# Four edits to the last stage of a two-layer kernel: where its scatters, its tile rows, its turned states and its filling products stand

## The chip, the cores and the metric

The kernel runs on one core of a Trainium2 chip. A core has a matrix engine (PE, with its weight loads listed apart as PEld), a vector engine (DVE), a scalar engine (ACT), a general engine (POOL) and an engine that only issues transfers (SP). Each works through its own instructions in order, and they wait for each other through semaphores. The metric is the device time of one execution in microseconds, as the median of several runs.

## The reference

The reference is a model of two layers on x of 8 x 512 x 256 (all fp32): conditioning, attention, a recurrence and a mixture of heads in the first, an adaptive low-rank block, causal attention, a second recurrence and a layer of experts in the second. Only the last two matter here; the input of this stage is x after everything else, and its output is added to x.

```python
# second recurrence: 512 steps, 8 rows, 256 states
xW = jnp.einsum('ntd,dh->nth', x, Wx) + b
def step(h_prev, xw_t):
    h_next = jnp.tanh(xw_t + h_prev @ Wh)
    return (h_next, h_next)
_, hs = jax.lax.scan(step, h0, jnp.swapaxes(xW, 0, 1))
x = jnp.swapaxes(hs, 0, 1)
# experts: 16, the best two of each row, and a shared one
router_logits = jax.nn.sigmoid(x @ gate_w + gate_b)
expert_values, expert_indices = jax.lax.top_k(router_logits, k=2)
expert_values = expert_values / jnp.sum(expert_values, axis=-1, keepdims=True)
hg = jnp.einsum('bsd,edi->bsei', x, experts_wg)
hu = jnp.einsum('bsd,edi->bsei', x, experts_wu)
all_outputs = jnp.einsum('bsei,eid->bsed', jax.nn.silu(hg) * hu, experts_wd)
selected = jnp.take_along_axis(all_outputs, expert_indices[..., None], axis=2)
return x + mlp(x, shared_wg, shared_wu, shared_wd) + jnp.sum(expert_values[..., None] * selected, axis=2)
```

## The kernel before

The last stage is the function `rnn_moe`. One loop over t = 0 to 511 emits a step of the recurrence and, beside it, a piece of the work on rows that are done. The order of PE, ACT and DVE is written out by that loop; the order of POOL and SP is left to the scheduler of the tile framework.

A step (`rnn_step`) is: 8 small products of the state with Wh into one of two accumulators `M.pg` (L1446; the 256 outputs stand in four strips of 32 partitions, 64 columns each, so the four run side by side); the tanh on ACT (L1448); a turn of 32 x 32 blocks on DVE into a ring of 16 steps (L1449), which is the state operand of the next step. `rnn_seed` (L1430) starts the next accumulator with the projected input: it picks the 8 rows of step t+1 with columns of the identity, four products. All seeds stand on PE between the state products of one step and those of the next, and behind the other products of that step.

Beside a step the loop calls four queues of generators, each advanced by one `yield` in a step. `ranks` and `gathers` are advanced in every step. Of `chunks` and `big` one is advanced: `chunks` first, and `big` if that gave 0. A `yield 1` says that products were emitted, a `yield 0` that none were. A step in which both give 0 is called empty here; in it the seeds are emitted three times in place of once.

What the queues hold, in order of time:

- `rnn_project` (`big`, first 62 steps): the projections x @ Wx of 16 steps, one 256-wide product in a step (L1411).
- `chunk` (every 16 steps): 128 finished rows. POOL copies the ring into hT; two turns pass; then logits of the router and the turned states `hr` (L1500, L1502), the shared expert (L1516, L1525, L1538) and the residual (L1542).
- `rank` (after 9, 9, 9 and 5 chunks, a block): sorts the rows by expert, with each expert's rows in whole tiles of 128; then 18 scatters of a block (10 in the last), each an indirect DMA from POOL of 128 rows of `hr` into `M.xs` (L1627). Each is ordered behind the turn of the step in which it is emitted (`paced`). After four more turns `tiles` goes into `big`.
- `tiles`: 33 tiles in a block (25 in the last). `fetch` copies an expert's weights on POOL (L1657, L1658) and loads 128 rows from `M.xs` on SP (L1660); the first four are fetched at once, the others four tiles ahead. A tile takes three steps: two gate products (L1673), then the down product of the tile before (L1689) with the turn of the rows two tiles on (L1665). The results go to `M.ys` (L1694).
- `collect`: indirect DMAs from POOL that gather rows from `M.ys` (L1725), their weighted sum (L1733) and the output. There is one gather in every three or four steps, and after the loop two in three.

When the loop over t ends, what is left in the queues is emitted without steps in between: the tail. M.pace, behind which gathers and scatters are ordered, is then the last down product.

Of the kernel before, what the change touches and what calls it, by code (L numbers as in the profile page):

```python
# [10 lines left out]
F32 = mybir.dt.float32  # L11
I32 = mybir.dt.int32
U32 = mybir.dt.uint32
AF = mybir.ActivationFunctionType
# [5 lines left out]
P = 128  # L20
B = 8
S = 512
D = 256
# [51 lines left out]
def load_kp(nc, pool, src, name, n, k=2, eng=None):  # L75

    t = pool.tile([P, k, n], F32, name=name)
    (eng or nc.sync).dma_start(out=t, in_=src.rearrange("(k p) n -> p k n", p=P))
    return t
# [295 lines left out]
class Edges:  # L375
# [3 lines left out]
    NE = E // P  # L379
# [1000 lines left out]
XB = 16  # L1380
# [42 lines left out]
        yield 0  # L1423


def rnn_seed(K, M, t, closed=False):

    pick = K.ident.rearrange("p (b t) -> p t b", b=B)
    for j in range(4):
        K.nc.tensor.matmul(  # L1430
            M.pg[t % 2][32 * j : 32 * j + B], pick[:, t % XB, :], M.xw[:, t // XB, 64 * j : 64 * j + 64], start=True, stop=closed
        )


def rnn_step(K, M, t):


    nc, mm = K.nc, K.nc.tensor.matmul
    at = t % XB
    if at == 0:  # L1440
        M.last, M.ring = M.ring, M.rg.tile([P, XB, 2, 32], F32, name="ring", tag="ring")
    pg = M.pg[t % 2]
    for k in range(2):
        hp = K.h0T[:, k, :] if t == 0 else (M.ring[:, at - 1, k, 0:B] if at else M.last[:, XB - 1, k, 0:B])
        for j in range(4):
            mm(pg[32 * j : 32 * j + B], hp, M.wh[:, k, 64 * j : 64 * j + 64], start=False, stop=(k == 1))  # L1446
    h = M.hp.tile([P, 64], F32, name="h", tag="h")
    nc.scalar.activation(h, pg, AF.Tanh)  # L1448
    M.pace = nc.vector.transpose(M.ring[:, at].rearrange("p k b -> p (k b)"), h)  # L1449


class Experts:
# [9 lines left out]
    NE = 16  # L1462
# [20 lines left out]
    def chunk(self, c, ring):  # L1483

        K, M, NE = self.K, self.M, self.NE
        nc, mm, later = K.nc, K.nc.tensor.matmul, M.later
        t0 = (self.first + c) * XB
        hT = M.hp.tile([P, 2, B, XB], F32, name="hT", tag="hT")
        for k in range(2):
            nc.gpsimd.tensor_copy(hT[:, k], ring[:, :, k, 0:B].rearrange("p t b -> p b t"))  # L1490
        for n in range(2):
            saved_x(K, M, t0 // XB + n)
        xc = M.saved[t0 // XB]
        hk = [hT[:, k].rearrange("p b t -> p (b t)") for k in range(2)]
        yield 0
        yield 0
        ph = M.pd.tile([P, D + NE], F32, name="ph", tag="pd")
        pr, pt = ph[:, D : D + NE], ph[:, 0:D]
        for k in range(2):
            mm(pr, hk[k], M.wr[:, k, :], start=(k == 0), stop=(k == 1))  # L1500
        for k in range(2):
            nc.tensor.transpose(pt[:, k * P : (k + 1) * P], hk[k], K.ident)  # L1502
        rl = M.sp.tile([P, NE], F32, name="rl", tag="rl")
        hr = M.ap.tile([P, D], F32, name="hr", tag="hr", bufs=16)
        self.hr.append(hr)

        def turned():
            nc.vector.tensor_tensor(rl, pr, M.rb, ALU.add)
            nc.scalar.activation(rl, rl, AF.Sigmoid)
            nc.scalar.copy(hr, pt)  # L1510

        later(turned)
        yield 1
        pw = M.pgu.tile([P, 2, P], F32, name="pw", tag="gu")
        for k in range(2):
            mm(pw[:, 0], M.wg[:, k, :], hk[k], start=(k == 0), stop=(k == 1))  # L1516

        def first():
            nc.vector.max(out=self.top[:, c, :], in_=rl)
            nc.vector.max_index(out=self.topi[:, c, :], in_max=self.top[:, c, :], in_values=rl)  # L1520

        later(first)
        yield 1
        for k in range(2):
            mm(pw[:, 1], M.wu[:, k, :], hk[k], start=(k == 0), stop=(k == 1))  # L1525
        a = M.sp.tile([P, P], F32, name="a", tag="a")

        def act():
            nc.scalar.activation(a, pw[:, 0], AF.Sigmoid)
            nc.vector.tensor_tensor(a, pw[:, 0], a, ALU.mult)  # L1530
            nc.vector.tensor_tensor(a, pw[:, 1], a, ALU.mult)

        later(act)
        yield 1
        yield 0
        yield 0
        pd = M.pd.tile([P, D], F32, name="pd", tag="pd")
        mm(pd, a, M.wd, start=True, stop=False)  # L1538
        yield 1
        pj = pd.rearrange("p (j k r) -> p k j r", j=4, k=2)  # L1540
        for k in range(2):
            mm(pj[:, k], xc[:, k], K.ident, start=False, stop=(k == 1))  # L1542
        acc = M.ap.tile([P, D], F32, name="acc", tag="acc", bufs=27)
        self.acc.append(acc)
        later(
            lambda: nc.vector.tensor_tensor(
                acc.rearrange("p (j k r) -> p j k r", j=4, k=2),
                pd.rearrange("p (j k r) -> p j k r", j=4, k=2),
                hr.rearrange("p (k j r) -> p j k r", j=4, k=2),
                ALU.add,  # L1550
            )
        )
        yield 1

    def rank(self):

        K, M, NE, NT, C, rp, top = self.K, self.M, self.NE, self.NT, self.C, self.rp, self.top
        nc, mm = K.nc, K.nc.tensor.matmul
# [66 lines left out]
        for c in range(C):  # L1625
            for i in range(2):
                w = nc.gpsimd.indirect_dma_start(  # L1627
                    out=self.xs[:, :],
                    out_offset=bass.IndirectOffsetOnAxis(ap=self.row[:, c, i : i + 1], axis=0),
                    in_=self.hr[c],  # L1630
                    in_offset=None,
                )
                self.paced(w)
                K.tc.declare_no_dep(w.ins, group=group, reason="rows of their own")
                K.tc.add_to_no_dep_group(group, w.ins)
                yield 0

    def tiles(self):

        K, M, NT = self.K, self.M, self.NT  # L1640
        nc, mm, later = K.nc, K.nc.tensor.matmul, M.later
# [11 lines left out]
        def fetch(m):  # L1653
            if m % 4 == 0:
                whose(m)
            e, W[m] = bass.ds(W[m], 1), M.wp.tile([P, 768], F32, name="w", tag="w")
            nc.gpsimd.tensor_copy(W[m][:, 0 : 2 * D], M.wgu[:, e, :].rearrange("p o n -> p (o n)"))  # L1657
            nc.gpsimd.tensor_copy(W[m][:, 2 * D : 3 * D], M.wdn[:, e, :].rearrange("p o n -> p (o n)"))  # L1658
            X[m] = M.sp.tile([P, D], F32, name="x", tag="x", bufs=6)
            nc.sync.dma_start(out=X[m], in_=self.xs[m * P : (m + 1) * P, :])  # L1660
# [36 lines left out]

        for m in range(4):
            fetch(m)
        for m in range(2):  # L1700
            turn(m)
            yield 1
# [38 lines left out]
def rnn_moe(K, out):  # L1741


    nc, inp = K.nc, K.inp
    with ExitStack() as es:
        wp = K.pool(es, "m_w")
# [13 lines left out]
        M.wh = load_kp(nc, wp, inp["rnn_wh"], "wh", 256)  # L1760
        M.rbias = wp.tile([P, D], F32, name="rbias")
        nc.sync.dma_start(out=M.rbias, in_=inp["rnn_b"].partition_broadcast(P))
        M.wr = load_kp(nc, wp, inp["gate_w"], "wr", 16)
        M.rb = wp.tile([P, 16], F32, name="rb")
        nc.sync.dma_start(out=M.rb, in_=inp["gate_b"].partition_broadcast(P))
        M.wg = load_kp(nc, wp, inp["shared_wg"], "wg", P)
# [19 lines left out]
        M.hp = K.pool(es, "m_h", 2)  # L1786
        M.psx = K.pool(es, "m_px", 1, PSUM)
        psg = K.pool(es, "m_pg", 1, PSUM)
        M.pg = [psg.tile([P, 64], F32, name=f"pg{i}") for i in range(2)]
        for t in M.pg:  # L1790
            nc.vector.memset(t, 0.0)
        M.pxt = K.pool(es, "m_xt", 1, PSUM)
        M.pgu = K.pool(es, "m_gu", 2, PSUM)
        M.pd = K.pool(es, "m_pd", 2, PSUM)
# [27 lines left out]

        def ranked(x):
            yield from x.rank()
            for _ in range(4):
                yield 0
            big.append(tiled(x))

# [11 lines left out]
        with K.tc.manual_schedule(engines={E.PE, E.Activation, E.DVE}):  # L1840
            for t in range(S):
                if t % XB == 0:
                    if t == XB * sum(BLOCKS[: nb + 1]):
                        nb += 1
                        block, at = Experts(K, M, nb), 0
                rnn_step(K, M, t)
                consume()
                advance(ranks)
                advance(gathers)
                idle = not (advance(chunks) or advance(big))  # L1850
                if t + 1 < S:
                    for i in range(2 * idle, -1, -1):
                        rnn_seed(K, M, t + 1, i > 0)
                if t % XB == XB - 1:
                    chunks.append(chunk(block, at, M.ring))
                    at += 1
            while chunks or ranks or big or gathers:
                consume()
                M.left = bool(chunks or ranks or big)
                advance(ranks)  # L1860
                advance(gathers)
                if advance(chunks) or advance(big):
                    M.pace = M.last
            consume()
# [171 lines left out]
```

## Time and profile before

| | |
|---|---|
| median of 10 runs | 4029.07 us (4020.14 to 4034.01) |
| the profiled execution | 4028.14 us, span 4026.0 us |
| the last stage's loop, first to last turn (L1449) | 3227.42 to 3881.91 us |
| the tail | 3881.91 to 4026 us |
| busy in the whole span | PE 3517.3, PEld 2437.5, DVE 2337.2, ACT 1523.4, POOL 666.7 us |
| mean granted PE clock | 0.976 |

How to read it: a busy time is that of an engine with an instruction in it; PE's records overlap, since matmuls are pipelined and their ends are modelled, so the start of one record to the start of the next is the better measure. An fp32 product of the common form stands as two records, a transpose as one. A line of the timeline has the start and the duration in us, the engine, the line of the kernel, the operation with its output and inputs, how many records were merged, and in brackets the idle time before it and what ended that. In a table by stretch the columns are the stretch, its length, the busy time of each engine with the number of instructions, the granted PE clock (1.00 is full speed), the busy share of the DMA engines and GB/s.

### The profile page before, as it was taken

To read this page: it belongs to the slowest core of one execution; us is meant where nothing else is said; L and a number is where in the kernel's file an instruction comes from. 1 tells how busy PE (TensorE), PEld (TensorE's weight loads), DVE (VectorE), ACT (ScalarE), POOL (GpSimd) and SP (SyncE) were. 2 spreads that over 40 slices of the span, in tenths; PEclk is the share of its full clock that TensorE was granted. 3 is DMA by queue.
4 is the path that set the end of the run, shared out by engine and by line. 5 is a ranking of instruction groups with operands and counts; after the bars stand their busy time and mean duration, and the time that the engine had idled before them with its cause. 6 is when DMAs were issued, how large, how long until landed. Compare 5 with 4: busy or idle time off the path is not lost.

```text
span 4026.0 us, 152559 instructions
## 1 busy us (share of the span) xinstructions
PE 3517.3 (87%) x66340; PEld 2437.5 (61%) x66340; DVE 2337.2 (58%) x8334; ACT 1523.4 (38%) x5283; POOL 666.7 (17%) x1370
## 2 busy tenths in 40 slices
PE   8999888888888887599888999999998897898986
PEld 5533566666666666466555666666666665666665
DVE  4488666666666666466656666666666533233334
ACT  3111233334333333355444444444444322232333
POOL 1000000000000000111022222222222110233356
PEclk9999999999999999899999999999999999999998
DMA  3122000000000000100000000000000060222235
GB/s 107 43 72 70 24 16 21 21 16 16 5 4 4 4 4 33 55 17 25 2 1 1 1 1 1 1 1 1 1 1 1 1 197 31 68 67 89 73 121 152
DMA packets 100814, 138.13 MB, mean 34 GB/s; under 512 B 13152, under 2 KB 81664, under 8 KB 99760
## 3 DMA queue, kind: packets, MB, share of 16 engines
q1 hardware_dynamic: 85264, 88.80, 7.1%
q0 software_dynamic: 12064, 34.34, 2.7%
q8 instruction: 520, 8.52, 0.9%
q10 hardware_dynamic: 2816, 5.24, 0.4%
q14 instruction: 150, 1.23, 0.1%
HBM read 86.26 MB, written 43.25 MB: 32 GB/s over the span
## 4 chain that ended last, share of the span: by engine, by line
PE 65%; DVE 17%; ACT 12%; issue 4%; DMA 1%; POOL 1%; another core or an unknown queue 0%; SPq 0%; POOLq 0%; ACTq 0%; DVEq 0%
PE pgi L669 8%; PE pe L1223 4%; PE pg L1446 4%; PE pp L1183 4%; DVE G L675 4%; PE pt L1266 3%; PE po L1281 3%; PE U L489 3%; PE pg L1673 3%; PE px L1298 3%; PE pk L468 3%; ACT X L676 3%; ACT th L686 3%; DVE pr L682 2%; PE pg L1430 2%
## 5 line engine op out<-in xcount | busy, mean ns | idle before, releaser
L669 PE MATMUL pgi<-wh,ring 128*8 128x128 f32 x8176 | 318.6, 274 | 207.6 <-DVE ring L687 206.8
L669 PEld LDWEIGHTS pgi<-wh,ring 128*8 128x8 f32 x8176 | 171.2, 88 | 378.3 <-DVE ring L687 377.7
L1449 DVE STREAM_TRANSPOSE ring<-h 128x64 f32<-128x64 f32 x512 | 125.6, 245 | 424.4 <-ACT h L1448 410.6
L1243 ACT ACTIVATE sm<-sm,nm 128x388 f32<-128x388 f32 (+3 forms) x512 | 284.0, 556 | 175.0 <-DVE nm L1239 174.6
L676 ACT ACTIVATE X<-G 128x32 f32<-128x32 f32 x512 | 117.1, 229 | 597.1 <-DVE G L675 597.1
L675 DVE STREAM_TRANSPOSE G<-pgi 128x128 f32<-128x128 f32 x512 | 162.7, 318 | 233.5 <-PE pgi L669 233.5
L1448 ACT ACTIVATE h<-pg 128x64 f32<-128x64 f32 x512 | 114.7, 224 | 481.4 <-PE pg L1446 421.8
L1183 PE MATMUL pp<-hn,wqkv 128*128 128x512 f32 x512 | 251.3, 636 | 30.4 <-ACT oT L1282 29.5
L1446 PE MATMUL pg<-wh,ring 128*8 128x64 f32 x8176 | 215.3, 223 | 62.5 <-DVE ring L1449 50.3
L1266 PE MATMUL pt<-ident,sm 128*128 128x128 f32 x1280 | 189.9, 281 | 74.0 <-DVE sm L1249 61.7
L1250 POOL COPY pme<-sm 128x4 f32<-128x4 f32 x512 | 120.3, 235 | 759.5 <-DVE sm L1249 755.6
L1266 PEld LDWEIGHTS pt<-ident,sm 128*128 128x128 f32 x1280 | 147.8, 143 | 155.2 <-issue 93.7
L1268 ACT COPY eT<-pt 128x512 f32<-128x512 f32 (+1 forms) x192 | 105.6, 550 | 352.4 <-PE pt L1266 351.0
L630 POOL COPY xc<-xT 128x128 f32<-128x128 f32 x64 | 17.1, 296 | 1184.5 <-DVE xT L552 1184.5
L669 PE MATMUL pgo<-wh,ring 128*8 128x64 f32 x8176 | 208.1, 219 | 1.9 <-issue 1.9
L669 PE MATMUL pgg<-wh,ring 128*8 128x64 f32 x8176 | 207.7, 219 | 0.0
L648 PE MATMUL pgi<-xw,ident 128*8 128x128 f32 x4096 | 206.2, 273 | 0.0
L1239 DVE CUSTOM_DVE_ANT_0 sm<-pe,mask 128x260 f32<-128x260 f32 (+2 forms) x384 | 141.7, 425 | 90.0 <-PE pe L1223 89.7
L1446 PEld LDWEIGHTS pg<-wh,ring 128*8 128x8 f32 x8176 | 137.3, 91 | 87.3 <-DVE ring L1449 71.7
L1183 PEld LDWEIGHTS pp<-hn,wqkv 128*128 128x128 f32 x512 | 97.9, 201 | 150.3 <-issue 101.5
L636 PE MATMUL px<-wx,xc 128*128 128x256 f32 x512 | 178.7, 433 | 5.0 <-POOL xc L630 5.0
L1673 PE MATMUL pg<-xT,w 128*128 128x128 f32 x992 | 166.4, 300 | 18.6 <-issue 7.3
(496 smaller groups left out, 8148.5 us busy)
## 6 DMA issues: line engine op xcount, KB each, us to landing
cb<-order POOLq DMA_DIRECT2D x32, 512.0 KB
x<-xs SPq DMA_DIRECT2D x124, 128.0 KB
ys<-y SPq DMA_DIRECT2D x124, 128.0 KB
xs<-zero SPq DMA_DIRECT2D x66, 128.0 KB
w<-in_ada_w_dram SPq DMA_DIRECT2D x16, 512.0 KB
w<-in_moh_w_dram SPq DMA_DIRECT2D x32, 192.0 KB
xres<-xp SPq DMA_DIRECT2D x32, 128.0 KB
xc<-xres SPq DMA_DIRECT2D x32, 128.0 KB
```

What stands on the lines that cost most here:

```text
L636: mm(px, xc[:, k], wx[:, k, c], start=(k == 0), stop=(k == 1))
L648: mm(dst[32 * j : 32 * j + B], pick[:, t % XB, :], xw[:, j * 256 + lo : j * 256 + hi], start=True, stop=False)
L669: mm(dst[32 * j : 32 * j + B], hp, wh[:, k, j * 256 + lo : j * 256 + hi], start=False, stop=(k == 1))
L675: nc.vector.transpose(G[:, 0:2].rearrange("p g k b -> p (g k b)"), pgi[t % 2].rearrange("p g n -> p (g n)"))
L676: nc.scalar.activation(X[:, 0:2], G[:, 0:2, :, 0:B], AF.Sigmoid)
L1183: mm(pp, T.wqkv[:, k, 0 : 2048].rearrange("p (i g h n) -> p i g h n", i=2, g=4, h=2)[:, i, g, h], self.hn[b][:, k, :], start=(k == 0), sto ...
L1223: mm(pe[a][:, 0 : w - lo], q[r, h, at], k[r, h, lo:w], start=(h == 0), stop=(h == 1))
L1239: nc.vector.tensor_tensor_reduce(out=sm[a][:, lo:w], in0=pe[a][:, 0 : w - lo], in1=T.mask[:, S - n + lo : 4 + S], scale=-1.0 / 8.0, scalar ...
L1243: nc.scalar.activation(sm[a][:, 0:w], sm[a][:, 0:w], AF.Exp, bias=nm[:, a : a + 1], scale=-1.0, accum_out=su[:, a : a + 1])
L1266: nc.tensor.transpose(pt[:, at, :], sm[i * m + a][:, 4 + j * P : 4 + (j + 1) * P], K.ident)
L1446: mm(pg[32 * j : 32 * j + B], hp, M.wh[:, k, 64 * j : 64 * j + 64], start=False, stop=(k == 1))
L1673: mm(pg, W[m][:, k * D + g * P : k * D + (g + 1) * P], X[m][:, k, :], start=(k == 0), stop=(k == 1))
```

## The change

Four edits, all in the last stage.

1. After the second scatter of a chunk one more turn passes, so that there are two scatters in three steps; after the last one six turns pass where four did.
2. `tiles` lets five turns pass between its first four fetches and the first turned rows.
3. Logits and turned states come from two products in place of four. The router's weights `M.wr` stand beside an identity: the first half of the states is multiplied by [identity, weights], the second by [weights, identity], and the two overlap in the 16 columns of the logits. The copy to `hr` reads around these columns.
4. In an empty step two 256-wide products of the identity with Wx, into columns of the next accumulator that nothing reads, stand ahead of the seeds, and the seeds are emitted once in place of three times. The accumulators `M.pg` are 320 columns wide for it.

```diff
-def rnn_seed(K, M, t, closed=False):
+def rnn_seed(K, M, t):
 
     pick = K.ident.rearrange("p (b t) -> p t b", b=B)
     for j in range(4):
         K.nc.tensor.matmul(
-            M.pg[t % 2][32 * j : 32 * j + B], pick[:, t % XB, :], M.xw[:, t // XB, 64 * j : 64 * j + 64], start=True, stop=closed
+            M.pg[t % 2][32 * j : 32 * j + B, 0:64], pick[:, t % XB, :], M.xw[:, t // XB, 64 * j : 64 * j + 64], start=True, stop=False
         )
...
-        pr, pt = ph[:, D : D + NE], ph[:, 0:D]
-        for k in range(2):
-            mm(pr, hk[k], M.wr[:, k, :], start=(k == 0), stop=(k == 1))
-        for k in range(2):
-            nc.tensor.transpose(pt[:, k * P : (k + 1) * P], hk[k], K.ident)
+        pr = ph[:, P : P + NE]
+        mm(ph[:, 0 : P + NE], hk[0], M.wr[:, 0], start=True, stop=False, skip_group_check=True)
+        mm(ph[:, P : D + NE], hk[1], M.wr[:, 1], start=False, stop=True, skip_group_check=True)
...
-            nc.scalar.copy(hr, pt)
+            nc.scalar.copy(hr.rearrange("p (k n) -> p k n", k=2), bass.AP(ph.tensor, ph.offset, [list(ph.ap[0]), [P + NE, 2], [1, P]]))
...
                 K.tc.add_to_no_dep_group(group, w.ins)
-                yield 0
+                for _ in range(1 + i):
+                    yield 0
...
         for m in range(4):
             fetch(m)
+        for _ in range(5):
+            yield 0
         for m in range(2):
             turn(m)
             yield 1
...
-        M.wr = load_kp(nc, wp, inp["gate_w"], "wr", 16)
+        M.wr = wp.tile([P, 2, P + 16], F32, name="wr")
+        for k in range(2):
+            nc.sync.dma_start(out=M.wr[:, k, P - k * P : P - k * P + 16], in_=inp["gate_w"][k * P : (k + 1) * P, :])
+            nc.gpsimd.tensor_copy(M.wr[:, k, k * 16 : k * 16 + P], K.ident)
...
-        M.pg = [psg.tile([P, 64], F32, name=f"pg{i}") for i in range(2)]
+        M.pg = [psg.tile([P, 64 + D], F32, name=f"pg{i}") for i in range(2)]
...
             yield from x.rank()
-            for _ in range(4):
+            for _ in range(6):
                 yield 0
             big.append(tiled(x))
...
                 idle = not (advance(chunks) or advance(big))
                 if t + 1 < S:
-                    for i in range(2 * idle, -1, -1):
-                        rnn_seed(K, M, t + 1, i > 0)
+                    if idle:
+                        for k in range(2):
+                            nc.tensor.matmul(M.pg[(t + 1) % 2][:, 64 : 64 + D], K.ident, M.wx[:, k, :], start=True, stop=True)
+                    rnn_seed(K, M, t + 1)
```

More of the change, by code (lines that the diff above doesn't have):

```diff
@@ L1445, in rnn_step @@
         for j in range(4):
-            mm(pg[32 * j : 32 * j + B], hp, M.wh[:, k, 64 * j : 64 * j + 64], start=False, stop=(k == 1))
+            mm(pg[32 * j : 32 * j + B, 0:64], hp, M.wh[:, k, 64 * j : 64 * j + 64], start=False, stop=(k == 1))
     h = M.hp.tile([P, 64], F32, name="h", tag="h")
-    nc.scalar.activation(h, pg, AF.Tanh)
+    nc.scalar.activation(h, pg[:, 0:64], AF.Tanh)
     M.pace = nc.vector.transpose(M.ring[:, at].rearrange("p k b -> p (k b)"), h)
@@ L1788, in rnn_moe @@
         psg = K.pool(es, "m_pg", 1, PSUM)
-        M.pg = [psg.tile([P, 64], F32, name=f"pg{i}") for i in range(2)]
+        M.pg = [psg.tile([P, 64 + D], F32, name=f"pg{i}") for i in range(2)]
         for t in M.pg:
-            nc.vector.memset(t, 0.0)
+            nc.vector.memset(t[:, 0:64], 0.0)
         M.pxt = K.pool(es, "m_xt", 1, PSUM)
```

## The prediction

> **What bounds it.** The change touches only the last stage, the second recurrence and its expert layer. The granted clock and the core's span came first (one core, mean clock 0.976), then the busiest groups of instructions. The profiled execution took 4028.14 us, 4026.0 of them span and 2.1 around it; the median of the ten runs is 4029.07. My sum is made against 4028.1, and 0.9 is added at the end.
>
> ```profile
> span 4026.0 us, 152559 instructions
> L1449 DVE STREAM_TRANSPOSE ring<-h 128x64 f32<-128x64 f32 x512 | 125.6, 245 | 424.4 <-ACT h L1448 410.6
> ```
>
> 512 steps run in a ring: state product (L1446), tanh (L1448, 0.22 us), turn (L1449), next state product. The first turn starts at 3227.42, the last at 3881.91: 654.5 us, 1.28 a step. From there to 4026 is a tail of 144 us in which only tiles, gathers and scatters are left. The timeline shows the shortest step, an empty one:
>
> ```profile
> 3389.58 0.24 DVE L1449 STREAM_TRANSPOSE ring<-h 128x64 f32<-128x64 f32 x1 [1.66 <-ACT h L1448]
> 3389.88 0.41 PE L1446 MATMUL pg<-wh,ring 128*8 128x64 f32 x16 [0.33 <-DVE ring L1449]
> 3390.11 0.52 PE L1430 MATMUL pg<-xw,ident 128*8 128x64 f32 x24
> 3390.36 0.22 ACT L1448 ACTIVATE h<-pg 128x64 f32<-128x64 f32 x1 [0.88 <-PE pg L1446]
> 3390.61 0.24 DVE L1449 STREAM_TRANSPOSE ring<-h 128x64 f32<-128x64 f32 x1 [0.79 <-ACT h L1448]
> ```
>
> It lasts 1.03 us and PE waits for the ring: its 24 seed records are through long before. Steps with products between L1446 and the seeds go by PE's own queue instead. PE's timeline, a projecting step and one with a down product and two turned rows:
>
> ```profile
> 3258.82 0.70 PE L1411 MATMUL px<-wx,xp 128*128 128x256 f32 x2
> 3259.45 0.30 PE L1430 MATMUL pg<-xw,ident 128*8 128x64 f32 x8
> 3259.57 0.41 PE L1446 MATMUL pg<-wh,ring 128*8 128x64 f32 x16
> 3259.91 0.70 PE L1411 MATMUL px<-wx,xp 128*128 128x256 f32 x2
> ...
> 3501.75 0.70 PE L1689 MATMUL py<-w,ea 128*128 128x256 f32 x2
> 3502.28 0.38 PE L1665 MATMUL pt<-ident,x 128*128 128x128 f32 x2
> 3502.60 0.30 PE L1430 MATMUL pg<-xw,ident 128*8 128x64 f32 x8
> 3502.72 0.41 PE L1446 MATMUL pg<-wh,ring 128*8 128x64 f32 x16
> ```
>
> Start to start, one 256-wide product holds PE 0.63 (3258.82 to 3259.45), seeds 0.12, L1446 0.34: 1.09, which is the step. With 0.85 of products (3501.75 to 3502.60) it is 1.31. So a step lasts max(1.03, 0.46 + products).
>
> The third reading is where steps are long. Busy time of L1449 by stretch (its count is the number of steps): empty and shared-expert work, then the scatters of the first three blocks.
>
> ```profile
> 3322.75:3389.58 66.83, 14.71 (x61) 1.00 0.08 26
> 3414.92:3449.64 34.72, 4.41 (x18) 0.80 0.21 74
> 3597.21:3633.06 35.85, 4.42 (x18) 0.86 0.25 87
> 3796.53:3833.20 36.67, 4.42 (x18) 0.81 0.26 88
> ```
>
> Plain steps take 1.1; the 18 steps with a scatter each take 1.93 to 2.04, at a clock of 0.80 to 0.86. The timelines of POOL and ACT at the first two scatters show how:
>
> ```profile
> 3415.50 1.04 POOL L1627 DMA_INDIRECT xs<-hr,row  x1 [8.24 <-DVE ring L1449]
> 3417.64 1.00 POOL L1627 DMA_INDIRECT xs<-hr,row  x1 [0.46 <-DVE ring L1449]
> ...
> 3416.85 0.22 ACT L1448 ACTIVATE h<-pg 128x64 f32<-128x64 f32 x1 [1.97 <-PE pd L1542]
> 3418.23 0.22 ACT L1448 ACTIVATE h<-pg 128x64 f32<-128x64 f32 x1 [1.16 <-PE pg L1446]
> ```
>
> The state product's records end at 3415.68, yet its tanh starts at 3416.85, 0.3 after POOL is done with the indirect DMA. The first such step takes 2.19, the second 1.38, and the next, in which no scatter starts, 1.06. The other blocks begin alike: 2.11 and 1.36, 2.13 and 1.38. Gathers (L1725), one in three steps or more, cost as a first one each time: 36 steps with 11 of them take 51.23 us (3677.26 to 3728.49), 0.9 over plain for each. In all 79 indirect DMAs start inside the recurrence, 54 scatters and 25 gathers.
>
> **The change part by part.** Which step holds what follows from the instructions as built: steps with no chunk or tile work rise from 72 to 90. Of the 90, 57 come before the first scatter (all empty before too), 22 lie in the 27 steps of the first block's scatters, 11 elsewhere, where tile work stood.
>
> *Wide products.* An empty step drops 8 seed products (16 of 24 records) and gains two 256-wide products ahead of the seeds. The first costs 0.63; the second adds its two records, 0.43 by the gap of 0.21 between the 256-wide records in PE's records. 0.46 + 1.06 = 1.52 instead of 1.03, +0.48. Bounds: 0, were they to fit into PE's 0.6 of waiting, and 0.69, were the second to cost as much as the first. I take 0.48: the 1.31 row has three of the same four records. Queued behind them are the seeds and the next L1446, so tanh and turn wait too. 57 x 0.48 = +27.4; the 11 empty steps elsewhere replace tile steps of 1.17 on average: 11 x 0.35 = +3.9.
>
> *Scatters, two in three steps.* A scatter still waits for a turn; behind it on POOL stand the copies of the states (hT) and of the weights, which the chunk's first product and the gate products wait for. That product has waited 1.6 us for hT in total so far; up to 2 more are left to the range. For the step times I take the pairs that started fresh: 2.15, 1.40, then a plain step. First block, 27 steps: before 34.72 + 10.8 for the nine that followed = 45.5; after, 9 x 2.15 + 18 x 1.52 (the wide pair covers the 1.40) = 46.7: +1.2. Second and third: before 35.85 + 36.67 + 18 x 1.17 = 93.6; after 18 x (2.15 + 1.42 + 1.17) = 85.3: -8.3. Bounds: no gain, if a scatter keeps its 0.86 excess, and -24 more, if it costs nothing.
>
> The Trainium skill, page "SBUF — State Buffer", section "Who interferes with whom", says that PE and ACT wait for no other engine's port use and that a DMA does not contend with compute. By it the scatters would not be what lengthens these steps, spacing them would gain nothing, and the sum below would be about 8 higher; the 1.17 us of late tanh beside POOL's indirect DMA is against it, without showing the path.
>
> *Logits and turned states in two products.* Four products hold PE from 3408.89 to 3409.70, 0.81; two 128-wide fp32 products hold it 0.64 (3410.16 to 3410.80), and 16 more columns add some 0.03. -0.145 each, 31 in the recurrence: -4.5. The strided read of the 354 ns copy changes neither its size nor its engine. Bounds: 0 and -6, with what the next step gains.
>
> *Rows asked for five turns ahead, two turns more after the scatters.* The gate products of the first three blocks start 17, 24 and 32 steps later than before. Six gathers leave the recurrence: 6 x 0.9 = -5.4. Waits for rows and low clock at a block's first tiles, steps of 1.5 against 1.1 to 1.3, go: -2 (bounds 0 and -5). SP has the same loads, earlier.
>
> *Setup.* Two copies of the identity on POOL (0.29 each by the xp copies) and one more small load lie behind work that waits 4.13 us for the bias. Nothing; at most 0.6 if that cover went.
>
> *The tail.* 58 tiles instead of 54 end there, 232 instead of 210 gate products, and 45 gathers instead of 39. Where no gather runs, a tile takes 1.55 (L1689 at 3932.56 and 3934.10); where one runs, POOL sets 2.31 for a gather and a weight copy (3974.65 to 3976.96), of which a copy is 1.0. So 5 x 1.55 = 7.8 by PE, 5 x 1.0 + 6 x 1.3 = 12.8 by POOL. Against it: spread scatters of the last block may shorten PE's waits of 4.44 and 2.84 after 3911. I take +9, bounds +1 and +13.
>
> Sum: 27.4 + 3.9 + 1.2 - 8.3 - 4.5 - 5.4 - 2 + 9 = +21.3. 4028.1 + 21.3 + 0.9 = 4050.
>
> **Rivals.**
> The other side: the wide products hide. For it, PE waits 0.33 before each L1446 and ends its seeds early. Then 68 x 0.48 goes and the first block's plain steps shorten too, -37: 4013, faster. It decides where a pair costs less than some 0.20 us. The 1.31 row, in which the same queue is not hidden, speaks against it.
>
> Scatters with room cost almost nothing: -24 for the second and third blocks, -6 for the first: 4020. For it, the second of a pair costs 0.3 only. Against it, a gather after two free steps still costs 0.9.
>
> The spacing doesn't take: POOL's order as built puts several weight copies ahead of the first scatters and bunches them up, as in the steps of 3.8 us before. Then 8 to 10 come back and the tail costs 13: 4063; with late hT copies 4066.
>
> **How the numbers follow.** Forecast, 4037 to 4060: 0.60. Spacing without effect, 4060 to 4078: 0.15. Scatters cheap or a tail without loss, 4015 to 4037: 0.18. Hidden pairs, near 4013: 0.07. Ten percent off at each end gives 4027 to 4067. One measurement tells 0.2% (8 us) from no change: above 4037 lies 0.75; of the rest some 0.12 ends below 4021, 0.13 between.
>
> **What would show it.** Right: the steps before the first scatter at 1.5 with wide products on PE and a clock of 1.00; first scatters of a pair near 2.15, second near 1.4 to 1.5; the turned-states step at 1.13; the last turn near 3894 and a tail above 150. Wrong: empty steps at 1.03 to 1.1, scatter steps under 1.3, or a tail no longer than 144.

## The result and the profile after

The changed kernel takes 4048.20 us (median of 9 runs, 4044.04 to 4053.39), the kernel before, in runs beside it, 4028.99 (30 runs): a ratio of 1.0051, 95% interval 1.0043 to 1.0060. The change costs some 20 us; 4050 was predicted. The profiled execution took 4048.72 us.

The span and the turns, from the page of the changed kernel:

```profile
span 4046.8 us, 150877 instructions
L1449 DVE STREAM_TRANSPOSE ring<-h 128x64 f32<-128x64 f32 x512 | 125.6, 245 | 437.1 <-ACT h L1448 425.4
```

The span is 20.8 longer. To see where, the 511 steps are cut by their number at the starts of L1449, in both traces alike:

| stretch | before, us | after, us | difference | predicted |
|---|---|---|---|---|
| up to the first turn | 3227.4 | 3229.1 | +1.7 | 0 |
| 82 steps before the first scatters (steps 85 to 167) | 91.0 | 115.2 | +24.1 | +27.4 |
| 27 steps, first block's scatters | 45.5 | 44.2 | -1.3 | +1.2 |
| 27 steps, second block's scatters | 46.1 | 44.0 | -2.1 | -8.3 for this row and the next |
| 27 steps, third block's scatters | 46.7 | 41.5 | -5.2 | see the row above |
| all other steps (348) | 425.2 | 419.8 | -5.5 | -8.0 |
| the tail | 144.1 | 153.2 | +9.1 | +9 |

The -8.0 holds the predicted +3.9, -4.5, -5.4 and -2. The table by stretch of the changed kernel, L1449 alone, shows the stretches with their clock (columns: stretch, its length, DVE busy and steps, granted PE clock, DMA share, GB/s; the first is the projecting steps, the last the tail):

```profile
3229.10:3325.11 96.01, 20.85 (x86) 0.98 0.61 199
3325.11:3440.28 115.17, 20.13 (x83) 1.00 0.05 15
3440.28:3484.44 44.16, 6.62 (x27) 1.00 0.18 61
3622.49:3666.48 43.99, 6.63 (x28) 0.96 0.26 89
3818.78:3860.24 41.46, 6.62 (x27) 1.00 0.30 101
3893.63:4046.80 153.17, 0.24 (x1) 0.91 0.55 163
```

In the second line the clock is full and the steps are still long. Their timeline says why; a step with the wide products:

```profile
3381.07 0.24 DVE L1449 STREAM_TRANSPOSE ring<-h 128x64 f32<-128x64 f32 x1 [1.27 <-ACT h L1448]
...
3381.74 0.31 PE L1430 MATMUL pg<-xw,ident 128*8 128x64 f32 x8
...
3381.86 0.41 PE L1446 MATMUL pg<-wh,ring 128*8 128x64 f32 x16
...
3382.20 0.70 PE L1858 MATMUL pg<-wx,ident 128*128 128x256 f32 x2
3382.33 0.22 ACT L1448 ACTIVATE h<-pg 128x64 f32<-128x64 f32 x1 [1.30 <-PE pg L1446]
3382.59 0.24 DVE L1449 STREAM_TRANSPOSE ring<-h 128x64 f32<-128x64 f32 x1 [1.27 <-ACT h L1448]
```

1.52 from turn to turn. The turn is over at 3381.31, the next L1446 begins at 3381.86: PE no longer waits for the ring as in the empty step of before, but is still at the wide products and the seeds. The scatters show the pairs that were reckoned with; the second block's first two, PE, POOL and ACT:

```profile
3622.84 0.41 PE L1446 MATMUL pg<-wh,ring 128*8 128x64 f32 x16
3623.01 0.99 POOL L1625 DMA_INDIRECT xs<-hr,row  x1 [1.50 <-DVE ea L1682]
...
3623.18 0.71 PE L1540 MATMUL pd<-ident,xc 128*128 128x128 f32 x4
...
3623.82 0.31 PE L1430 MATMUL pg<-xw,ident 128*8 128x64 f32 x8
3624.35 0.22 ACT L1448 ACTIVATE h<-pg 128x64 f32<-128x64 f32 x1 [1.73 <-PE pd L1540]
...
3625.13 0.97 POOL L1625 DMA_INDIRECT xs<-hr,row  x1 [1.13 <-DVE ring L1449]
3625.71 0.22 ACT L1448 ACTIVATE h<-pg 128x64 f32<-128x64 f32 x1 [1.14 <-PE pg L1446]
```

The turns stand at 3622.49, 3624.60, 3625.96 and 3627.00: steps of 2.11, 1.36 and 1.04. The first tanh comes 0.35 after the end of the indirect DMA, at 3624.00. In the third block all nine pairs go this way (2.10 to 2.23, then 1.35 to 1.46, then a step of 1.03 to 1.10). In the second block four of the nine do not: in three of them both scatters start in one step, which takes 2.55 to 3.24, and one pair takes 1.61 and 2.97.

### The profile page after: what moved, and what is told of

Same layout as the page of the kernel before. It is cut to its first block, busy times and chain, and to the rows that moved or that the text cites. A ratio compares the mean times of both kernels' runs of the same rounds, so it can differ in the third digit from the quotient of the medians.

```text
span 4046.8 us, 150877 instructions
## 1 busy us (share of the span) xinstructions
PE 3569.0 (88%) x65484; PEld 2468.0 (61%) x65484; DVE 2336.0 (58%) x8334; ACT 1523.6 (38%) x5283; POOL 666.7 (16%) x1372
## 4 chain that ended last, share of the span: by engine, by line
PE 66%; DVE 16%; ACT 11%; issue 4%; POOL 1%; DMA 1%; SPq 0%; POOLq 0%; another core or an unknown queue 0%; ACTq 0%; DVEq 0%
PE pgi L669 8%; PE pe L1223 4%; DVE G L675 4%; PE pg L1446 3%; PE pp L1183 3%; PE pt L1266 3%; PE po L1281 3%; PE U L489 3%; PE px L1298 3%; PE pk L468 3%; PE pg L1672 3%; PE pg L1430 3%; ACT X L676 3%; ACT th L686 3%; DVE pr L682 2%
## 5 line engine op out<-in xcount | busy, mean ns | idle before, releaser
L1449 DVE STREAM_TRANSPOSE ring<-h 128x64 f32<-128x64 f32 x512 | 125.6, 245 | 437.1 <-ACT h L1448 425.4
L1446 PE MATMUL pg<-wh,ring 128*8 128x64 f32 x8176 | 209.2, 220 | 32.7 <-DVE ring L1449 24.1
L1249 DVE TENSOR_SCALAR sm<-sm,rc 128x388 f32<-128x388 f32 (+3 forms) x512 | 175.9, 387 | 9.0
```

Source lines behind the costliest of these rows:

```text
L1249: nc.vector.tensor_scalar(sm[a][:, 0:w], sm[a][:, 0:w], rc[:, a : a + 1], None, ALU.mult)
L1446: mm(pg[32 * j : 32 * j + B, 0:64], hp, M.wh[:, k, 64 * j : 64 * j + 64], start=False, stop=(k == 1))
```

## The experiments

Twelve runs, of eleven further kernels and of the changed one again, in the order of the questions. "Stretch" is the one of 82 steps before the first scatters, which holds no indirect DMA.

### What the filling of the empty steps costs

The changed kernel with the triple seeds of before, the other edits kept:

```diff
-                    if idle:
-                        for k in range(2):
-                            nc.tensor.matmul(M.pg[(t + 1) % 2][:, 64 : 64 + D], K.ident, M.wx[:, k, :], start=True, stop=True)
-                    rnn_seed(K, M, t + 1)
+                    for i in range(2 * idle, -1, -1):
+                        rnn_seed(K, M, t + 1, i > 0)
```

> The changed kernel with the filling of before (seeds three times in an empty step), all other edits kept. Queue theory: like the kernel with no filling, within 4 us of it, 4010 to 4016: 37 us less than the changed kernel, since 24 seed records fit into PE's wait. Clock theory: some 10 to 25 us faster than with no filling, if the seeds hold the clock.

Measured: 4018.55, ratio 0.9967 (0.9954 to 0.9980). The stretch is 90.2, the recurrence 637.1 in place of 664.5. Its three scatter stretches take 42.8, 47.0 and 42.5, together 5.9 less than in the kernel before (138.2). A stretch alone says little: the second block's, with the same spacing, takes 44.0 in the changed kernel and 47.0 here, each in a single execution.

The kernel before with the wide products alone (the same lines the other way, with the wider accumulators):

> The kernel before with the wide products alone (edit 4). Queue theory: 57 empty steps ahead of the scatters at +0.49 give +28, the 15 in the first block's scatter steps little, since these wait for tanh anyway, +0 to +4: 4057 to 4061. Rival, in which the edits only cost together (the wide pair is dear because the spacing makes more empty steps): +10 or less, 4039.

Measured: 4056.15, ratio 1.0059 (1.0045 to 1.0074); stretch 115.6, empty steps 1.520. The 27 steps of the first block's scatters take 45.7, as before (45.5): there the wide products cost nothing. The whole of the loss is this one edit; the three others together gain. In the recurrence it costs the same with and without them: 27.3 alone (681.8 against 654.5) and 27.4 beside them (664.5 against 637.1). The whole times add up less well (1.0059 x 0.9967 is 1.0026, and the change is at 1.0051); where the rest lies is not located.

The changed kernel with nothing in place of the wide products:

```diff
-                    if idle:
-                        for k in range(2):
-                            nc.tensor.matmul(M.pg[(t + 1) % 2][:, 64 : 64 + D], K.ident, M.wx[:, k, :], start=True, stop=True)
                     rnn_seed(K, M, t + 1)
```

> The changed kernel without any filling in empty steps: the seeds once, no wide products. Queue theory (the wide pair costs because it stands on PE ahead of the next state product): empty steps fall from 1.52 to 1.03, the stretch of steps 85 to 167 from 115 to 91 us, and the time from 4048 to 4010 to 4015, below the kernel before. Clock theory (filling is paid for by a higher granted clock, and without it the clock drops to 0.5 in empty steps): the state product takes 0.6 in place of 0.4 us there, empty steps last 1.25 or more, the stretch lasts 105 or more and the time stays above 4025.

Measured: 4034.32, ratio 1.0010 (1.0002 to 1.0019), 16 more than with triple seeds; the stretch is 102.0. The table by stretch of this kernel, for the stretch and for four pieces of it:

```profile
3323.30:3425.30 102.00, 20.11 (x83) 0.77 0.04 12
3361.00:3371.10 10.10, 2.44 (x10) 1.00 0.06 16
3371.20:3381.30 10.10, 1.72 (x7) 0.50 0.01 2
3381.40:3391.50 10.10, 2.21 (x9) 1.00 0.05 16
3391.60:3401.80 10.20, 1.72 (x7) 0.50 0.01 2
```

And of the kernel with triple seeds:

```profile
3324.80:3415.00 90.20, 20.11 (x82) 1.00 0.07 20
```

The theory that only PE's queue counts falls, and with it the picture of the filling as dead weight: without it the clock alternates between 1.00 and 0.50, some 10 us each, and is low in the second half of a run of empty steps and in the steps with work that follow. What the bare kernel loses there lies little in the empty steps, which take 1.24 at the low clock and 1.03 at the full one (1.11 on average). The state product's records grow too, on the timeline of PE:

```profile
3369.89 0.41 PE L1446 MATMUL pg<-wh,ring 128*8 128x64 f32 x16 [0.51 <-DVE ring L1449]
...
3373.26 0.61 PE L1446 MATMUL pg<-wh,ring 128*8 128x64 f32 x16 [0.41 <-DVE ring L1449]
```

The most is lost in the steps with work behind them: turned states 2.02 against 1.15 with triple seeds, the shared expert's gate and up products 1.69 against 1.13 (means of 5 and 10 steps). So some filling pays, if it holds the clock and fits.

One wide product in an empty step:

```diff
-                        for k in range(2):
+                        for k in range(1):
                             nc.tensor.matmul(M.pg[(t + 1) % 2][:, 64 : 64 + D], K.ident, M.wx[:, k, :], start=True, stop=True)
```

> Changed kernel with one wide product in each empty step, not two. Theory, a step lasts 0.46 plus the products that stand ahead of the seeds, and never less than 1.03: one 256-wide product holds PE 0.63, so an empty step lasts 1.09 in place of 1.52, and the stretch of 82 steps before the first scatters falls from 115.2 to 92 to 95, at a clock of 1.00. The time is some 29 to 33 below that of the changed kernel: a ratio to the kernel before of 0.997 to 0.9985. Rival: one product keeps TensorE less busy than the triple seeds did, the clock falls as in the kernel without filling (0.74 there, steps of 1.25), the stretch takes 98 to 102 and the ratio is 0.999 to 1.001. Rival, the second product was the cheap one: steps above 1.25 at a full clock, ratio above 1.0005.

Measured: 3957.28 where the kernel before took 3972.41 (another chip, see below): ratio 0.9962 (0.9948 to 0.9976). Empty steps take 1.088, the stretch 91.2 at a clock of 1.00. An empty step of it on the timeline:

```profile
3350.96 0.24 DVE L1449 STREAM_TRANSPOSE ring<-h 128x64 f32<-128x64 f32 x1 [0.84 <-ACT h L1448]
...
3351.21 0.30 PE L1430 MATMUL pg<-xw,ident 128*8 128x64 f32 x8
...
3351.34 0.41 PE L1446 MATMUL pg<-wh,ring 128*8 128x64 f32 x16
...
3351.67 0.70 PE L1858 MATMUL pg<-wx,ident 128*128 128x256 f32 x2
```

The turn ends at 3351.20 and L1446 follows at 3351.34: PE is behind the ring by a hair only. Two products, one, three seeds and none give 1.52, 1.09, 1.03 and 1.24 (at the low clock). The first three are max(1.03, 0.46 + products), at a full clock.

### The two products

The kernel before with edit 3 alone (two products for logits and turned states, the copy around them, `M.wr`):

> The kernel before with logits and turned states from two products alone (edit 3). Queue theory: PE is held 0.67 in place of 0.81 us, the step goes from 1.27 to 1.13, 31 times: -4 to -5, 4024 to 4025. Rival (the step is set by hT from POOL or by the logits' way through DVE and ACT): no change, 4029.

Measured: 4023.15, ratio 0.9981 (0.9973 to 0.9990), 7.7 less. Turned-states steps go from a median of 1.272 to 1.147, which is 31 x 0.125 = 3.9; the recurrence shrinks by 3.7 (654.5 to 650.8). The rest lies outside it, in a first turn 3.2 earlier and a tail 2.9 shorter, and compares two single executions; it is not located.

### Spacing and asking ahead, each alone, on another chip

The kernel before with edit 1:

```diff
-                yield 0
+                for _ in range(1 + i):
+                    yield 0
...
-            for _ in range(4):
+            for _ in range(6):
```

> Kernel before with the spacing of the scatters alone (two in three steps, and two turns more after them); seeds, logits and requests for rows stay as they were. My theory, by pairs of about 2.15 and 1.4 with a step without a scatter behind them: the 27-step stretches of the second and third blocks, 46.1 and 46.7 in the kernel before, fall to 42 to 44 each and the first block's from 45.5 to 43; the start of the tiles moves back by 11 steps or so, which takes one or two gathers out of the recurrence and makes the tail 2 to 4 longer. In all 3 to 8 us faster, 4023 to 4027 where the kernel before has 4030. Rival, a scatter keeps its excess whatever stands around it: stretches of 46, the tail longer, 4031 to 4034.

Measured: 3960.07 beside 3974.70 for the kernel before: ratio 0.9963 (0.9950 to 0.9977), 14.6 less. And with edit 2 alone:

```diff
             fetch(m)
+        for _ in range(5):
+            yield 0
         for m in range(2):
```

> Kernel before with the rows asked for five turns ahead alone; scatters, seeds and logits stay as they were. My theory: steps of 1.5 at each block's first tiles go (-2), some gathers leave the recurrence for the tail (-3), and the tail gets 3 to 6 longer, since the last tiles start later too: 4028 to 4032, no difference from the kernel before (4030). Rival, the waits for rows at a block's first tiles cost much more than the trace shows: 4024 or less, with the recurrence 8 or more shorter. Rival the other way: the tail alone grows, by 8 or more, 4037.

Measured: 3982.28, ratio 1.0016 (1.0007 to 1.0025), slower. The tail is 153.5, against 146.5 with the spacing alone; the kernel before has no profile on this chip, and 144.1 on the first. So most of the change's longer tail is edit 2.

The kernel before took 4030.8 beside the kernels with triple seeds, wide products, no filling and two products, and 3974.7 beside these, 56 us less, on another chip. The step times show what differs: with the spacing, an otherwise empty step with a scatter in it takes 1.03 to 1.2 there, not 2.15, and the 27-step stretches take 30.0, 32.3 and 32.4. So I compare only with the kernel before on the same chip. Spacing still gains, and more than on the first chip: the three stretches take 110.8 with edit 2 alone, whose scatters are those of before, and 94.8 with the spacing, 16.0 less. Why is to be seen in the former; POOL, PE and ACT in one step of the first block:

```profile
3421.20 0.99 POOL L1627 DMA_INDIRECT xs<-hr,row  x1 [0.17 <-DVE ring L1449]
...
3422.49 0.97 POOL L1627 DMA_INDIRECT xs<-hr,row  x1 [0.30 <-issue]
3423.76 0.96 POOL L1627 DMA_INDIRECT xs<-hr,row  x1 [0.30 <-issue]
3425.03 0.97 POOL L1627 DMA_INDIRECT xs<-hr,row  x1 [0.30 <-issue]
3425.99 0.74 POOL L1490 COPY hT<-ring 128x128 f32<-128x128 f32 x2
...
3426.45 1.04 PE L1500 MATMUL ph<-wr,hT 128*128 128x16 f32 x4 [4.95 <-POOL hT L1490]
...
3428.82 0.22 ACT L1448 ACTIVATE h<-pg 128x64 f32<-128x64 f32 x1 [7.03 <-PE pg L1446]
```

One scatter after the other takes POOL 1.27 (3422.49 to 3423.76), and a step only 1.03 to 1.1. One in every step is more than POOL can do; scatters pile up, the copy of the states hT stands behind them, and the logits, which need it, hold up the whole of PE for 4.95: a step of 7.25, and of 5.23 and 4.84 in the other two blocks. With two scatters in three steps POOL keeps up, and these steps are 1.78, 1.50 and 1.50. On the first chip the steps, slowed by the late tanh, are mostly longer than POOL's 1.27, and hT was waited for 1.6 in all.

The changed kernel itself once more, on another chip, which turned out to be of this kind:

> The changed kernel itself once more, to see it on a chip where a tanh beside an indirect DMA is not late (if it comes to one; on one where it is, this is the first comparison again, 1.005). There, from the kernel with one wide product (ratio 0.9962, 15 less than the kernel before) plus the second product: 24 in the stretch before the first scatters (115 for 91.2), 8 in the first block's scatters (38 for 30), 3 in the twelve steps behind them: +20, a ratio of 1.0045 to 1.0055, 3991 to 3995 where the kernel before has 3972 to 3975. The change would so come to the same ratio on both chips by other terms: on the first chip the spacing gains 6 there and on this one some 20, on the first the wide products in the first block hide behind the late tanh, here they cost 8. Rival: what makes the scatters cheap on this chip also lets the wide products hide: stretch of 91, ratio below 1.000. Rival: the spacing gains less here, as scatters are cheap anyway: ratio above 1.007.

Measured: 3997.26 beside 3976.41, ratio 1.0056 (1.0042 to 1.0070). Its table by stretch, the same steps as above:

```profile
3316.75:3431.73 114.98, 20.13 (x82) 1.00 0.05 15
3431.73:3469.85 38.12, 6.63 (x28) 1.00 0.21 71
3607.90:3639.31 31.41, 6.62 (x28) 1.00 0.36 120
3776.67:3808.02 31.35, 6.63 (x28) 1.00 0.39 129
```

and its second block's first two scatters:

```profile
3608.42 0.98 POOL L1625 DMA_INDIRECT xs<-hr,row  x1 [1.49 <-DVE ea L1682]
3608.72 0.22 ACT L1448 ACTIVATE h<-pg 128x64 f32<-128x64 f32 x1 [0.69 <-PE pg L1446]
...
3609.70 0.97 POOL L1625 DMA_INDIRECT xs<-hr,row  x1 [0.30 <-issue]
3609.91 0.22 ACT L1448 ACTIVATE h<-pg 128x64 f32<-128x64 f32 x1 [0.97 <-PE pg L1446]
```

Here the tanh runs in the middle of the indirect DMA. In this execution no tanh beside an indirect DMA starts more than 0.5 after the end of the state product's records (110 of them, median 0.07); in the first execution of the same kernel 49 of 85 do (median 0.69). The recurrence is 620.7 here and 664.5 there, the tail the same (153.6 and 153.2).

The ratio is the same on both kinds of chip, and made of other terms, as expected: the stretch costs 24 on both; the first block's wide products hide there behind the late tanh (44.2 with them, 42.8 with triple seeds), and here they cost 8 (38.1, against 30.0 with one product); for it the spacing gains more here (16.0 in the three stretches, 5.9 there).

### What makes the tanh late

Two kernels were meant to tell. The changed kernel with plain transfers from POOL in place of the scatters:

```diff
-                w = nc.gpsimd.indirect_dma_start(out=self.xs[:, :], out_offset=..., in_=self.hr[c], in_offset=None)
+                n = 2 * c + i
+                w = nc.gpsimd.dma_start(out=self.xs[n * P : (n + 1) * P, :], in_=self.hr[c])
```

> Changed kernel with each of the 64 scatters replaced by a transfer of the same 128 rows, issued by POOL in the same place and behind the same turn, to fixed consecutive rows (the rows are so not sorted by expert, and the tiles' and gathers' values are not the reference's; the work of every engine but POOL's issue stays the same). Theory that the indirect DMA's own microsecond on POOL makes the tanh late: the 27-step stretches fall from 44.0 and 41.5 in the second and third blocks to 30 to 32 each, and in the first block to about 40, where the wide products set 1.52: about 25 less, 4020 to 4026. Rival, any transfer issued from POOL there makes the tanh late: stretches as in the changed kernel, 4046 to 4050. Between the two, a plain issue that is shorter on POOL (0.5 say) holds the tanh for as long as it lasts: 4034 to 4040.

This kernel leaves out the sorting of the rows by expert and so does not compute the reference. Measured: 3989.01 beside 3974.70, ratio 1.0032 (1.0019 to 1.0046). It came to a chip where the tanh is not late: its stretches, 38.1, 31.2 and 31.2, are those of the changed kernel on such a chip, and the question stays open. The rest of its difference lies in its tail (146.7), where rows of other places are worked on.

The kernel with triple seeds, with scatters and gathers ordered behind the state product:

```diff
-            mm(pg[32 * j : 32 * j + B, 0:64], hp, M.wh[:, k, 64 * j : 64 * j + 64], start=False, stop=(k == 1))
+            M.pace = mm(pg[32 * j : 32 * j + B, 0:64], hp, M.wh[:, k, 64 * j : 64 * j + 64], start=False, stop=(k == 1))
...
-    M.pace = nc.vector.transpose(M.ring[:, at].rearrange("p k b -> p (k b)"), h)
+    nc.vector.transpose(M.ring[:, at].rearrange("p k b -> p (k b)"), h)
```

> Changed kernel with the triple seeds of the kernel before in place of the wide products (4018.5 where the kernel before had 4030.8), and every scatter and gather made to wait for the last matmul of the step's state product, not for the turn that follows it some 0.5 us later. Theory: POOL's indirect DMA holds up the tanh that comes due while it runs, until about 0.4 after its end. Started some 0.5 earlier it ends 0.5 earlier, and the tanh of its own step has its inputs already: some 50 first indirect DMAs of the recurrence at 0.4 to 0.5 less each, -20 to -25, about 3996 to 4000; first scatter steps at 1.7 in place of 2.15. Rival: the tanh of the own step is caught as well, so that the late tanh moves one step ahead and nothing is gained: first scatter steps still 2.1 to 2.2, 4016 to 4022. Rival, both the own tanh and the next are late: 4030 or more.

Measured: 3961.29 beside 3974.70, ratio 0.9965 (0.9952 to 0.9979), on the chip of the last two: nothing was late there, so again it tells nothing of the cause. Its ratio is that of the kernel with one wide product on the same chip (0.9962), so nothing is seen of the pace either way.

The traces on record narrow the question. An engine's waits end with semaphore updates, and these are in the trace. In the changed kernel's first profile 67 state products have their last record end beside an indirect DMA. The update that PE owes the tanh then comes at least 0.36 later, in the median 1.06; in the 445 other steps it comes 0.04 later, and never more than 0.05. All but one of the late tanhs start 0.02 after an update from PE, as the prompt ones do, so ACT is not what is held up. PE itself goes on starting records meanwhile, as the lines of the second block's first scatter show (3623.18 and 3623.82, with the tanh at 3624.35). The step from ACT to DVE is not late: when the tanh ends beside an indirect DMA (21 times), the turn follows after 0.03, as elsewhere. On the other kind of chip PE's update beside an indirect DMA comes after 0.045 in the median (69 products). So what is late is the end of PE's product or its update; which of the two cannot be told, since the ends of PE's records are modelled.

### A version that beats both

The two edits that gained alone, in the kernel before:

> Kernel before with the two edits that gained by themselves: logits and turned states in two products, and scatters two in three steps with two turns more behind them. Seeds and requests for rows stay as they were. If the gains add, 0.9981 (two products) by 0.9963 (spacing): a ratio of 0.9945, 0.993 to 0.996, 22 us less than the kernel before of the same chip; turned-states steps 1.147, no step in which three or more indirect DMAs start, tail 143 to 148. On a chip where a tanh beside an indirect DMA comes a microsecond late, as in the first profiles, the spacing brings less (the 27-step stretches together 6 less than before) and the ratio is 0.9965. Rival: the gains overlap, because both shorten the same waits around the turned-states step, or the tail takes them back (above 152): 0.9965 or more on any chip.

Measured: 3954.50 beside 3972.41, ratio 0.9953 (0.9939 to 0.9968); the 0.9944 of both gains multiplied lies in the interval. The changed kernel with one wide product, 0.9962 in the same set, is not clearly behind it. The same with the other pace:

> The kernel with two products and spaced scatters (0.9953 of the kernel before), with every scatter and gather waiting for the last matmul of the step's state product and not for the turn behind it. On a chip where a tanh beside an indirect DMA is late until 0.4 after its end: the DMA ends up to 0.5 sooner, first scatter steps 1.7 in place of 2.15, a ratio of 0.985 to 0.990; or, the rival, the tanh of the own step is caught too and first scatter steps stay at 2.1 to 2.2, ratio 0.993 to 0.998. On a chip where it isn't late, the pace has nothing to gain: scatter steps 1.03 to 1.2 with both, a ratio of 0.9945 to 0.9965.

It came to a chip with a late tanh: 4013.78 beside 4032.25, ratio 0.9954 (0.9940 to 0.9967). So the pair of edits gains on both kinds of chip, here with the other pace. On the question of the tanh, the second block's first two scatters:

```profile
3598.12 0.41 PE L1446 MATMUL pg<-wh,ring 128*8 128x64 f32 x16
3598.32 0.98 POOL L1625 DMA_INDIRECT xs<-hr,row  x1 [0.15 <-ACT xT L1666]
3599.70 0.22 ACT L1448 ACTIVATE h<-pg 128x64 f32<-128x64 f32 x1 [1.43 <-PE pd L1540]
3599.95 0.97 POOL L1625 DMA_INDIRECT xs<-hr,row  x1 [0.64 <-PE pd L1540]
...
3601.37 0.22 ACT L1448 ACTIVATE h<-pg 128x64 f32<-128x64 f32 x1 [1.44 <-PE pg L1446]
```

In the three blocks the step of the first scatter takes 2.18, 2.20 and 2.14, as the rival said, but the edit hardly moved these scatters: a typical one starts 0.46 after the turn's start, 0.52 before, and the one shown starts when POOL is done with its copies. The second scatter did start 0.5 sooner, beside its step's turn. Its tanh then came 0.45 after its end, and the step took 1.71, 1.66 and 1.68, not 1.38. An earlier start is thus no cure, and the theory that the end of the DMA alone sets the tanh is not whole either: a second scatter in its old place lets the tanh through 1.1 after the turn, before its own end. Why PE's update is late stays open.

## Why the prediction was right

The sum gave +21.3 for a span that grew by 20.8, and the mechanism of its largest term is shown. That the sum is so close is partly luck: its terms missed by -3.3 (wide products), -2.5 and +1.0 (scatters), +2.5 (all other steps) and +1.7 (up to the first turn), and these cancel. It is luck too that the ratio holds on the other kind of chip, where the terms are others.

**Wide products**, +27.4: the price for each step was right, 1.033 to 1.520. The stretch grew by 24.1, since the 56 empty steps counted in it had taken 1.067 on average before, not 1.033 (now 1.514: +25.0), and its other steps gave some back (-1.1 in the shared expert's down products, -0.7 in the turned states, +0.9 elsewhere). One wide product alone at 1.088 shows the rule in a third point. The rival that a pair hides is out: it would have needed a stretch near 91.

**Scatters**, +1.2 and -8.3: measured -1.3 and -7.3. In the third block the working stands, pair by pair. In the second its total fits (44.0 for 42.7), though four of nine pairs went otherwise, and another execution with the same spacing took 47.0, so that part of the fit is chance. The 18 steps of before that were read as holding one scatter each held none, one or two. In the first block the 1.52 of the plain steps was laid beside the late steps, not behind them: a step without a scatter often took 1.03, since PE had done its wide products while the tanh was late, and the pair cost 1.4 in all (44.2 against 42.8 with triple seeds). And the row behind the term, 2.15 for a first scatter, belongs to the chip: on two others a scatter costs next to nothing. The bound "scatters with room cost almost nothing" was so met elsewhere, without its time: the wide products then lie open in the first block. The up to 2 left for late hT copies were not needed: no step of the changed kernel's scatters is longer than 1.59 there. What the working had not seen is that in the spacing of before these copies cost far more there (steps of 7.25, 5.23 and 4.84, against 1.78, 1.50 and 1.50), and most of the spacing's gain of 14.6 comes from these. The page "SBUF — State Buffer" of the Trainium skill, section "Who interferes with whom", which was set against the late tanh, agrees with the trace on those two chips (the tanh beside an indirect DMA 0.07 behind its product's records in the median) and not on the first kind (0.69, and it is PE's update that comes late).

**Two products**, -4.5: 31 x 0.125 = -3.9, a step's 0.145 having been a little too much; measured alone, -3.7 in the recurrence and -7.7 in the time.

**Rows ahead**, -5.4 and -2: the gathers in the recurrence fell from 25 to 18, seven and not six. All other steps together, where these terms lie with the +3.9 and most of the -4.5, gave -5.5 for the -8.0.

**Tail**, +9: measured +9.1. It outweighs what edit 2 gives: alone that edit is 0.16% slower, on a chip where a gather in the recurrence costs little.

**Setup**, 0: the first turn came 1.7 later, in one execution of each; with edit 3 alone it came 3.2 earlier. That is the scatter of single executions, and no cost of these loads can be read from it.

## What to carry to other kernels

Before filling an engine's empty time, find the length that fits: here a chain of 1.03 hid three seeds, a product of 0.63 lengthened it by 0.06, and 1.06 of products made PE's queue the bound; no filling at all let the clock fall to 0.50 for about half of the time and cost most in the steps behind. An engine that issues transfers one per step needs its own time per transfer to be under the step, or they pile up in front of something else in its queue. A cost read beside one kind of instruction should be looked for on a second chip before it is built on: the total can agree while its terms don't.

## What the runs showed of the hardware

- Chips differ by a mechanism, not only by a scale: the kernel before took 4029 to 4032 us in three sets of runs and 3972 to 3976 in three others. For the changed kernel's 52 us (spans of 4046.8 and 3995.0), 44 lie in the recurrence, where the tanh beside an indirect DMA is late or not; 8 lie ahead of it and were not looked into.
- With gaps of only 0.5 us ahead of each state product, PE's granted clock fell to 0.50 after some ten steps, and then alternated between 1.00 and 0.50, about 10 us each; 16 more seed records of 8 columns by 64, or one 256-wide product, in each empty step held it at 1.00.
- On the chips with the longer times, PE's semaphore update for a state product that ends beside POOL's indirect DMA came late: by 0.82 to 1.09 us in the medians of four profiles (64 to 67 products each), against 0.04 elsewhere, while the step from ACT to DVE stayed at 0.03. On the two others it came after 0.045 to 0.074 in the medians of four profiles.
